# The last stage of a two-layer transformer kernel: choosing tokens in four partition quadrants and in two halves

## The chip, the cores and the metric

The kernel runs on one core of a Trainium2 chip. The core has five engines, each with its own instruction stream, worked in order: PE (TensorE, matmuls and transposes), DVE (VectorE), ACT (ScalarE), POOL (GpSimd) and SP (SyncE, which here only issues DMAs). They wait for each other by semaphores. The metric is device microseconds of one execution. The kernel before took 2501.3 us, the median of 3 runs (2497.42 to 2508.35).

## The reference

Four sequences of 1024 tokens with 256 features go through two layers. Layer 0 (windowed attention, then a feed-forward network with two of eight experts per token) and the attention of layer 1 (16 heads, normalised output) matter here only because they run before. The change is in the feed-forward part of layer 1, where experts choose tokens:

```python
gate_logits = jnp.einsum('bnd,de->bne', x, gate_w)
competitive_gates = sinkhorn(gate_logits)            # 8 rounds over tokens, then over experts
vals, idx = jax.lax.top_k(jnp.swapaxes(competitive_gates, -1, -2), M)   # M = 1024 / 8 = 128
...
routed = x[b_idx, routed_indices]
outputs = jnp.einsum('ebmd,edf->ebmf', routed, experts)                 # 8 experts, 256 x 256
outputs = outputs * jnp.transpose(gate_values, (2, 0, 1))[..., None]
routed_back = jnp.zeros_like(x).at[b_idx, routed_indices].set(vals_bmed)
```

Here x is the layer-normalised input, and the result is added to the input. Each of 8 experts takes the 128 best tokens of each sequence. Where several experts take one token, one row remains: that with the highest slot number, among equals that of the highest expert.

## The kernel before

Tokens stand in 32 tiles of 128 (x_t). The sequences form two groups: group 0 has sequences 0 and 1 (tiles 0 to 15), group 1 has 2 and 3. A group has 16 rows of (sequence, expert) with 1024 gate values each. The steps for a group, with the functions that give them:

- gate_steps (L1014) normalises a tile (xng, L1024, on POOL), stores it to DRAM (xn_d, L1027) and computes its gate logits (transposes L1038, matmuls L1048, clip L1055).
- share_steps (L1064) does eight rounds of scaling by sums over tokens (matmul L1075) and over experts; all between are small DVE operations.
- choose_steps (L1088) turns the gates to 16 rows of 1024 (L1100) and then, 16 times, finds the eight largest (L1109), their positions (L1111) and overwrites them with -1 (L1115), all on DVE. Three long operations per round make 47 in all. The 128 values and positions are transposed into columns, one per (sequence, expert): slot_gate, slot_tok and slot_row (L1123 to L1130).
- experts_on (L1135) gathers the chosen rows of xn_d, 128 rows per gather, by indirect DMAs that POOL issues (L1143), transposes two at a time (L1181), copies them (ACT, L1185), multiplies by the expert (L1154), scales by the gate (ACT, L1164) and stores to DRAM (y_d, issued by SP, L1168). Six xg buffers.
- The ranks say which slot of which expert holds a token. For group 0 they are scattered to DRAM (rank_d, POOL, L1597, 16 DMAs) and read back (read_ranks, L1234). For group 1 they are made on the core: hot (DVE, L1832) is a row of ones and zeros, place == slot, and one-hot matmuls against slot_col (L1834) sum slot numbers into rank_ps.
- back (L1194) finds each token's row of y_d in eleven small DVE steps (L1202 to L1219), gathers the rows (POOL, L1225), adds x (L1231; on POOL for group 0, on DVE for group 1) and stores to the output (SP, L1232).

Group 0's gates, shares, choice and scatters run inside the attention loop of layer 1 (the loop over p, 32 pairs of heads, and k, 8 steps), a step at a time (some, L1624; step, L1615; the lists between, gating, sort and aside). In that loop the maxima of a later pair are made ahead (maxima, L1423: matmuls L1429, reduced on DVE to tops, L1436) and go through DRAM (tops_d, L1453, and back, L1458); scores (L1471), their exponential on ACT (pT, L1479) and the sums (L1486) follow. finish (L1540) normalises the attention's output tiles on POOL (L1559 to L1564). With lag 0, the call of the last tile, finish and gate_steps run without fill between.

After the loop, group 1's shares, choice, experts, ranks and back follow, with group 0's experts and back given beside the choice: the code takes three steps of choose, then experts_on(0), 24 more steps, back(0), and the rest of choose. Each engine's order is made when the kernel is built, by a list scheduler: among the instructions that its own model holds ready it takes the one that was given first. Hence the order in which the Python code gives the work, and the buffers it has, decide the order in each engine's stream; tc.issue_after and paced tie an instruction to the newest one of another engine. DMAs wait in the stream of the engine that issues them, so that a store that waits for its data holds up what stands behind it on SP.

## Time and profile before

| what | us |
|---|---|
| median of 3 runs | 2501.3 (2497.42 to 2508.35) |
| the profiled execution | 2505.83 |
| its span | 2504.1 |
| PE, DVE, ACT, POOL busy in the span | 2273.6, 1392.9, 985.6, 632.2 |
| last gates of group 1 clipped (L1055) | at 2357.18 |
| last share round ends, choice of group 1 begins (L1091) | at 2378.86 |
| first and last long operation of that choice | 2381.85, 2440.7 |
| group 1's gathers of xn_d, first and last issue | 2442.77, 2462.94 |
| group 1's gathers of y_d, first and last issue | 2477.94, 2497.00 |

The page's line of 40 slices shows which engine is busy where, in tenths, and the clock that the throttle granted PE:

```profile
PE   6999999799999999999888999999999999998434
DVE  5455545524321222222476877777777798995393
ACT  1333333312111222222114666666666565666311
POOL 2233333510440000000333221212122211124455
PEclk8999999899999999999999999999999999999667
```

One slice is 62.6 us, so the last three are the stage that the change is about. "Idle before" names the instruction that released an engine after an idle time; "issue" is time in which an engine waited for nothing that the profile shows. In the chain of what ended last, each row is a start, a duration and what ran.

### The profile page before, as it was taken

What the parts mean: (1) busy time and instruction counts of PE and PEld (TensorE: products, weight loads), DVE (VectorE), ACT (ScalarE), POOL (GpSimd) and SP (SyncE); (2) the same over time, 40 slices, a digit from 0 to 9 for tenths busy, and PEclk for the clock granted to TensorE, in tenths of its full rate; (3) what the DMA queues carried; (4) which work ended last, traced back from release to release, by engine and by line L of the source; (5) the groups of instructions that cost most, each with busy time, mean ns of one, the idle gap of its engine ahead of it and who ended that gap; (6) DMA issues with size and microseconds to landing.
All of it is one profiled execution on the core that took longest, in us unless ns stands there. A gap on an engine that the chain in (4) does not pass through costs nothing.

```text
span 2504.1 us, 42234 instructions
## 1 busy us (share of the span) xinstructions
PE 2273.6 (91%) x16844; PEld 1352.2 (54%) x16844; DVE 1392.9 (56%) x2304; ACT 985.6 (39%) x1354; POOL 632.2 (25%) x728
## 2 busy tenths in 40 slices
PE   6999999799999999999888999999999999998434
PEld 3566666566557888887444444444444444443222
DVE  5455545524321222222476877777777798995393
ACT  1333333312111222222114666666666565666311
POOL 2233333510440000000333221212122211124455
PEclk8999999899999999999999999999999999999667
DMA  3000000420116666664515221313121313100144
GB/s 93 19 11 11 11 13 9 133 74 1 66 63 200 217 206 209 213 207 156 117 44 120 59 69 45 69 45 69 45 69 45 69 44 69 44 19 11 56 122 135
DMA packets 201744, 204.90 MB, mean 82 GB/s; under 512 B 90200, under 2 KB 162392, under 8 KB 201548
## 3 DMA queue, kind: packets, MB, share of 16 engines
q1 hardware_dynamic: 179148, 162.13, 22.7%
q0 software_dynamic: 11584, 29.72, 4.0%
q10 hardware_dynamic: 10816, 10.36, 1.2%
q8 instruction: 133, 2.18, 0.4%
q14 instruction: 63, 0.52, 0.1%
HBM read 140.70 MB, written 56.96 MB: 79 GB/s over the span
## 4 chain that ended last, share of the span: by engine, by line
PE 69%; DVE 16%; issue 6%; ACT 4%; POOL 3%; DMA 3%; SPq 0%; DVEq 0%; ACTq 0%; POOLq 0%
PE two L962 10%; PE two L1471 9%; PE acc L1486 8%; PE two L717 6%; DVE tops L1436 5%; PE two L329 5%; PE two L1429 4%; PE acc L989 4%; PE two L258 3%; PE two L1351 2%; PE two L321 2%; PE acc L735 2%; PE misc L735 2%; PE acc L396 2%; PE misc L440 1%
## 5 line engine op out<-in xcount | busy, mean ns | idle before, releaser
L1436 DVE TENSOR_REDUCE tops<-two 128x2 f32<-128x1024 f32 x512 | 619.5, 1217 | 103.8 <-PE two L1429 101.6
L1479 ACT ACTIVATE pT<-two 128x1024 f32<-128x1024 f32 x512 | 523.4, 1025 | 303.7 <-PE two L1471 299.2
L1486 PE MATMUL acc<-pT,v_t 128*32 128x256 f32 x4096 | 342.7, 393 | 5.8 <-ACT pT L1479 5.6
L1471 PE MATMUL two<-q_st,k_st 64*128 64x512 f32 x1024 | 259.8, 499 | 19.3 <-ACT pT L1479 11.8
L962 PE MATMUL two<-xbT,w_t 128*128 128x256 f32 (+1 forms) x1280 | 260.0, 358 | 1.3 <-ACT xbT L951 0.7
L717 PE MATMUL two<-xnT_f,w_t 128*128 128x512 f32 x512 | 234.7, 608 | 7.4 <-DVE tops L1436 5.1
L962 PEld LDWEIGHTS two<-xbT,w_t 128*128 128x128 f32 x1280 | 224.1, 192 | 32.0 <-ACT xbT L951 5.3
L1429 PE MATMUL two<-k_st,q_st 64*128 64x512 f32 x1024 | 220.3, 403 | 4.2 <-DVE glu L726 1.6
L1471 PEld LDWEIGHTS two<-q_st,k_st 64*128 64x128 f32 x1024 | 96.8, 184 | 209.8 <-issue 118.8
L1659 POOL DMA_INDIRECT yr<-ys_d,slot x64 | 62.6, 979 | 573.5 <-DMA w_raw<-in_L_attn_wk_dram 434.7
L1471 PE MATMUL two<-top_st,minus 64*128 64x512 f32 x1024 | 206.5, 396 | 0.0
L978 DVE SCALAR_TENSOR_TENSOR glu_b<-two,b_blk,act_b 128x256 f32<-128x256 f32 (+1 forms) x160 | 72.6, 453 | 235.8 <-ACT act_b L972 235.8
L972 ACT ACTIVATE act_b<-two,b_blk 128x256 f32<-128x256 f32 (+1 forms) x160 | 72.1, 451 | 312.6 <-PE two L962 161.1
L1486 PEld LDWEIGHTS acc<-pT,v_t 128*32 128x32 f32 x4096 | 86.5, 108 | 166.1 <-issue 142.8
L717 PEld LDWEIGHTS two<-xnT_f,w_t 128*128 128x128 f32 x512 | 96.7, 195 | 116.4 <-issue 104.4
L989 PE MATMUL acc<-w_t,glu_b 128*128 128x256 f32 x568 | 148.6, 390 | 8.0 <-DVE glu_b L978 3.7
L355 DVE TENSOR_REDUCE top<-two 128x4 f32<-128x768 f32 (+1 forms) x128 | 112.5, 919 | 69.0 <-PE two L329 69.0
L381 POOL TENSOR_SCALAR_AFFINE_SELECT pT<-pT 128x1024 f32<-128x1024 f32 x64 | 70.5, 1102 | 296.5 <-ACT pT L378 296.5
L725 ACT ACTIVATE act<-two,bT 128x512 f32<-128x512 f32 x64 | 44.0, 687 | 254.0 <-PE two L717 251.2
L1429 PEld LDWEIGHTS two<-k_st,q_st 64*128 64x128 f32 x1024 | 103.2, 185 | 73.5 <-ACT pT L1479 22.0
L378 ACT ACTIVATE pT<-two 128x768 f32<-128x768 f32 (+1 forms) x128 | 93.7, 783 | 119.0 <-PE two L329 118.6
L989 PEld LDWEIGHTS acc<-w_t,glu_b 128*128 128x128 f32 x568 | 102.1, 189 | 34.7 <-DVE glu_b L978 23.3
(317 smaller groups left out, 3095.0 us busy)
## 6 DMA issues: line engine op xcount, KB each, us to landing
w_t<-in_L_ffn_rw_dram SPq DMA_DIRECT2D x120, 512.0 KB
halves<-split SPq DMA_DIRECT2D x64, 256.0 KB
q_st<-halves SPq DMA_DIRECT2D x128, 128.0 KB
k_st<-halves SPq DMA_DIRECT2D x256, 64.0 KB
xb<-xs_d SPq DMA_DIRECT2D x31, 256.0 KB
ys_d<-yb ACTq DMA_DIRECT2D x31, 256.0 KB
xs_d<-zeros SPq DMA_DIRECT2D x5, 1536.0 KB
b_t<-in_L_ffn_rb_dram SPq DMA_DIRECT2D x40, 128.0 KB
```

The costliest lines, as they stand in the source:

```text
L329: mm(parts[r][:, gg, :], lhsT=left[32 * r : 32 * r + rows, g, l0 : l0 + P], rhs=right[32 * r : 32 * r + rows, g, r0 : r0 + n], start=(mask ...
L355: nc.vector.tensor_reduce(tops[i][:, 2 * ab : 2 * ab + 2, 2 * gp : 2 * gp + 2], scs[ab], AX.X, ALU.max)
L378: nc.scalar.activation(pt[:, 2 * ab : 2 * ab + 2, :, :n], scs[ab], AF.Exp)
L717: mm(ps[:, n * 512 : (n + 1) * 512], lhsT=w_t[:, kc, f * P : (f + 1) * P], rhs=xnT[:, kc, cols], start=(kc == 0), stop=(kc == 1),)
L735: mm(ps[:, jj * D : (jj + 1) * D], lhsT=glu[:, f, j * P : (j + 1) * P], rhs=w3_t[:, f, :], start=(f == 0), stop=(f == NF - 1),)
L962: mm(ps[:, m * 512 + ff * cols : m * 512 + (ff + 1) * cols], lhsT=w_t[:, kc, f * P : (f + 1) * P], rhs=xbT[:, kc, :cols], start=(kc == 0), ...
L989: mm(ps[:, a * D : (a + 1) * D], lhsT=glu[:, f, a * P : (a + 1) * P], rhs=w3_t[:, f, :], start=(f == 0), stop=(f == NF - 1),)
L1429: mm(sc[:, hh], lhsT=q_st[rows, j * P : (j + 1) * P], rhs=k_st[rows, kk * 512 : (kk + 1) * 512], start=True, stop=True,)
L1436: newest["vector"] = nc.vector.tensor_reduce(tops[:, :, j, kk], sc, AX.X, ALU.max).ins
L1471: mm(sc[:, hh * 512 : (hh + 1) * 512], lhsT=minus[rows] if top else k_st[rows, k * P : (k + 1) * P], rhs=(top_ring[p % 2] if top else q_st ...
L1479: newest["scalar"] = nc.scalar.activation(pt, sc, AF.Exp).ins
L1486: newest["tensor"] = mm(oT_ps[32 * r : 32 * r + 32, hh * D : (hh + 1) * D], lhsT=vals[n // HU][:, n % HU, k, :], rhs=pts[r // 2][:, hh * 5 ...
```

## The change

- Choice: the gate rows are put twice on 32 partitions, and the work array has four column blocks on four quadrants of 32 partitions. Round k puts its eight values into quadrant k // 4, and writes the array with them replaced into the place of the next round, so that the array of each round stays. One lookup then finds positions for all quadrants of a column at once: four lookups for 16 rounds. With parts = 2 (group 1) the first half of the slots (64 per expert) is given after eight rounds, with four lookups of its own, and the second half after the last. The columns come from small matmuls; slot_gate is copied by ACT. A column of a half holds 64 slots each of two experts.
- Gathers: take_rows issues all rows of a group or half at once, from 16 xg buffers.
- Order after the loop: group 0's 16 gathers, group 1's share rounds, group 0's experts, the sources of group 0, then choose of group 1; after its first eight steps, six pieces of group 0's way back; after the first half of the choice, its gathers, half_experts and ranks; eight more pieces of the way back; the rest of the choice; the second half's gathers, two pieces, and per sequence the ranks, experts and way back.
- half_experts multiplies two half columns as 64-wide column tiles of PE, one expert each, and stores 64 rows at a time (32 stores instead of 16 for group 1).
- Ranks: the one-hot rows of the first half are made on ACT (Abs, then Relu), those of the second half on DVE; rank_ps, sources and back go by sequence.
- The last tile's finish and xng run on DVE instead of POOL (lag 0). Six yr0 buffers instead of seven.

```diff
--- before.py
+++ after.py
...
-            t = pool.tile([P, D], F32, tag="yr0", name="sb3_k", bufs=7)
+            t = pool.tile([P, D], F32, tag="yr0", name="sb3_k", bufs=6)
...
-            nc.gpsimd.tensor_scalar(
+            (nc.gpsimd if lag else nc.vector).tensor_scalar(
...
-    def choose_steps(g: int, bank, chosen, after):
-
-        by_tile = gpool.tile([P, TB, GE], F32, tag="by_tile", name="by_tile", bufs=1)
-        nc.vector.tensor_copy(
-            by_tile.rearrange("p t (b e) -> p t b e", b=GB),
-            gates[:, g * GT : (g + 1) * GT, :].rearrange("p (b t) e -> p t b e", b=GB),
-        )
+    def choose_steps(g: int, bank, chosen, after, parts: int = 1):
+        by_tile = gpool.tile([P, TB, 2, GE], F32, tag="by_tile", name="by_tile", bufs=1)
+        for n in range(2):
+            nc.vector.tensor_copy(
+                by_tile[:, :, n].rearrange("p t (b e) -> p t b e", b=GB),
+                gates[:, g * GT : (g + 1) * GT, :].rearrange("p (b t) e -> p t b e", b=GB),
+            )
         yield 0
+        cur = gpool.tile([P, 4, S], F32, tag="cur", name="cur", bufs=1)
...
+        for k in range(rounds):
+            q, a = of_round(k)
+            behind(nc.vector.max, out=top_v[q, a, :], in_=cur[q, a, :])
             yield 0
+            if k + 1 < rounds:
+                q1, a1 = of_round(k + 1)
+                behind(
+                    nc.vector.match_replace,
+                    out=cur[q1, a1, :], in_to_replace=top_v[q, a, :], in_values=cur[q, a, :],
+                    imm_value=-1.0,
+                )
                 yield 0
+            if (k + 1) % (rounds // parts):
+                continue
+            part = (k + 1) * parts // rounds - 1
+            rows = slice(part * P // parts, (part + 1) * P // parts)
+            for a in range(4):
+                behind(
+                    nc.vector.max_index,
+                    out=top_i[rows, a, :], in_max=top_v[rows, a, :], in_values=cur[rows, a, :],
+                )
+                yield 0
+            behind(nc.vector.tensor_copy, top_f[rows], top_i[rows])
+            ps = bank()
+            n = GE // parts
+            for k0, top in enumerate((top_v, top_f)):
+                for j in range(part * 4 // parts, (part + 1) * 4 // parts):
+                    q = slice(32 * j, 32 * j + 32)
+                    for h in range(parts):
+                        row = 64 * h + 32 * (j % 2) if parts == 2 else 32 * j
+                        mm(
+                            ps[row : row + 32, k0 * n : (k0 + 1) * n],
+                            lhsT=top[q].rearrange("p a i -> p (a i)"),
+                            rhs=ident[q, 32 * j + h : 32 * j + GE : parts],
+                            start=True,
+                            stop=True,
+                        )
+            slot_gate = gpool.tile([P, n], F32, tag=f"slot_gate{part}", name="slot_gate", bufs=1)
+            slot_tok = gpool.tile([P, n], F32, tag=f"slot_tok{part}", name="slot_tok", bufs=1)
+            slot_row = gpool.tile([P, n], I32, tag=f"slot_row{part}", name="slot_row", bufs=1)
+            nc.vector.tensor_copy(slot_tok, ps[:, n : 2 * n])
+            nc.vector.tensor_copy(slot_row, slot_tok)
+            nc.scalar.copy(slot_gate, ps[:, :n])
+            chosen[g, part] = slot_gate, slot_tok, slot_row
+            after()
+            yield 1
...
+    def half_experts(g: int, part: int, m: int, xgs, pool, w_all):
+        slot_gate = chosen[g, part][0]
+        xgT = turned(xgs, pool)
+        ps = two_banks()
+        for c in range(2):
+            for kc in range(2):
+                for h in range(2):
+                    half = slice(64 * h, 64 * h + 64)
+                    mm(
+                        ps[half, c * D : (c + 1) * D],
+                        lhsT=xgT[:, 2 * c + kc, half],
+                        rhs=w_all[:, (2 * (m + c) + h) % E, kc, :],
+                        start=(kc == 0),
+                        stop=(kc == 1),
+                    )
+        for c in range(2):
+            b = (m + c) // (E // 2)
+            yg = pool.tile([P, D], F32, tag="yg", name="yg", bufs=4)
+            nc.scalar.activation(
+                yg, ps[:, c * D : (c + 1) * D], AF.Copy, scale=slot_gate[:, m + c : m + c + 1]
+            )
+            for h in range(2):
+                row = ((2 * (m + c) + h) % E) * CAP + 64 * part
+                nc.sync.dma_start(
+                    out=y_d[g * GB + b][row : row + 64, :], in_=yg[64 * h : 64 * h + 64, :]
+                )
+    def sources(rank, n: int):
...
+        return src_row
+    def back(b: int, src_row, n0: int, adder, queue, rows):
+        for t in range(TB):
+            i = b * TB + t
+            yr = rows.tile([P, D], F32, tag="yr", name="yr", bufs=16)
             nc.gpsimd.indirect_dma_start(
                 out=yr[:, :],
                 out_offset=None,
+                in_=y_d[b][:, :],
+                in_offset=bass.IndirectOffsetOnAxis(ap=src_row[:, n0 + t : n0 + t + 1], axis=0),
+            )
+            adder.tensor_tensor(yr, yr, x_t[i], ALU.add)
             queue.dma_start(out=out_rows[i * P : (i + 1) * P, :], in_=yr)
+            yield
 
...
+                v = nc.gpsimd if lag else nc.vector
+                v.tensor_scalar(
                     ys[j], ys[j], mv[:, j, 0:1], rstd[:, j : j + 1], ALU.subtract, ALU.mult
                 )
-                nc.gpsimd.tensor_tensor(ys[j], ys[j], gamma_b, ALU.mult)
-                nc.gpsimd.tensor_tensor(ys[j], ys[j], beta_b, ALU.add)
-                nc.gpsimd.tensor_tensor(x, x, ys[j], ALU.add)
+                v.tensor_tensor(ys[j], ys[j], gamma_b, ALU.mult)
+                v.tensor_tensor(ys[j], ys[j], beta_b, ALU.add)
+                v.tensor_tensor(x, x, ys[j], ALU.add)
...
-            yr = pools["yr"].tile([P, D], F32, tag="yr0", name="yr0", bufs=7)
+            yr = pools["yr"].tile([P, D], F32, tag="yr0", name="yr0", bufs=6)
...
+        slot_col = wpool.tile([P, 2, E // 2, E], BF16, name="slot_col")
...
+        columns = [(n // E, n) for n in range(GE)]
+        xgs = take_rows(chosen[0, 0], columns, pool)
         run(share_steps(1, one_bank, 0))
+        experts_on(0, xgs, pool, w_all)
+        src_row = sources(read_ranks(), GT)
+        rest = iter(
+            [back(b, src_row, b * TB, nc.gpsimd, nc.sync, pool) for b in range(GB)]
+        )
+        def some_back(n: int, now=[next(rest)]):
+            with tc.issue_after(newest["rows"]):
+                while n and now:
+                    if next(now[0], now) is now:
+                        now[:] = [j for j in (next(rest, None),) if j]
+                    else:
+                        n -= 1
+        columns = [(GB + m // (E // 2), m) for m in range(E)]
+        rank_ps = two_banks()
+        ready = []
+        choose = choose_steps(1, one_bank, chosen, lambda: ready.append(0), 2)
+        def ranks_of(part: int, m: int, on_scalar: bool):
+            tok = chosen[1, part][1][:, m : m + 1]
+            hot = pool.tile([P, S], BF16, tag="hot", name="hot", bufs=3)
+            if on_scalar:
+                far = pool.tile([P, S], F32, tag="far", name="far")
+                nc.scalar.activation(far, place, AF.Abs, bias=minus_tok[:, m : m + 1])
+                nc.scalar.activation(hot, far, AF.Relu, bias=1.0, scale=-1.0)
+            else:
+                nc.vector.tensor_scalar(hot, place, tok, None, ALU.is_equal)
+            b, mb = divmod(m, E // 2)
+            for hf in range(2):
+                mm(
+                    rank_ps[32 * b : 32 * b + E, hf * 512 : (hf + 1) * 512],
+                    lhsT=slot_col[:, part, mb, :],
+                    rhs=hot[:, hf * 512 : (hf + 1) * 512],
+                    start=(part == 0 and mb == 0),
+                    stop=(part == 1 and mb == E // 2 - 1),
+                )
+        for _ in range(8):
             next(choose)
+        some_back(6)
+        while not ready:
             next(choose)
+        minus_tok = wpool.tile([P, E], F32, name="minus_tok")
+        nc.scalar.mul(minus_tok, chosen[1, 0][1], -1.0)
+        xgs = take_rows(chosen[1, 0], columns, pool)
+        for m in range(0, E, 2):
+            half_experts(1, 0, m, xgs[m : m + 2], pool, w_all)
+            for c in range(2):
+                ranks_of(0, m + c, True)
+            next(choose)
+        some_back(8)
         run(choose)
+        xgs = take_rows(chosen[1, 1], columns, pool)
+        some_back(2)
+        backs = []
+        for b in range(GB):
+            for m in range(b * E // 2, (b + 1) * E // 2, 2):
+                for c in range(2):
+                    ranks_of(1, m + c, False)
+                half_experts(1, 1, m, xgs[m : m + 2], pool, w_all)
+            mine = slice(32 * b, 32 * b + E)
+            rankT = pool.tile([P, S], F32, tag="rankT", name="rankT")
+            nc.scalar.copy(rankT[mine], rank_ps[mine, :])
+            ps = one_bank()
+            for t in range(TB):
+                nc.tensor.transpose(
+                    ps[:, t * E : (t + 1) * E], rankT[mine, t * P : (t + 1) * P],
+                    ident[mine, mine],
+                )
+            rank = gpool.tile([P, TB, E], F32, tag="rank1", name="rank1")
+            nc.scalar.copy(rank.rearrange("p n e -> p (n e)"), ps[:, : TB * E])
+            run(back(GB + b, sources(rank, TB), 0, nc.vector, nc.sync, pool))
```

169 lines of the change are left out of this document (57 added, 112 removed).

## The prediction

> **What bounds the kernel now.** I read the table of the span by stages first, the chain of what ended last second, then groups and timelines of single stages. The table's columns are stretch, its length, busy time of PE, weight loads, DVE, ACT and POOL, granted clock, DMA share, GB/s.
>
> ```profile
> 2010.00:2280.00 270.00, 254.59 (x2173) 118.21 (x2172) 246.09 (x336) 167.12 (x186) 49.48 (x59) 0.99 0.16 41
> 2280.00:2340.00 60.00, 48.70 (x391) 20.66 (x391) 11.14 (x32) 42.71 (x49) 39.32 (x43) 0.92 0.06 15
> 2340.00:2358.00 18.00, 9.28 (x31) 6.58 (x32) 5.26 (x24) 2.19 (x6) 9.42 (x13) 0.50 0.30 93
> 2358.00:2381.00 23.00, 6.23 (x24) 4.73 (x24) 14.60 (x49) 0.00 (x0) 4.75 (x5) 0.50 0.21 66
> 2381.00:2442.00 61.00, 20.20 (x99) 16.92 (x99) 59.09 (x83) 11.07 (x24) 36.01 (x42) 0.67 0.42 125
> 2442.00:2478.00 36.00, 29.54 (x136) 18.39 (x135) 13.87 (x28) 12.02 (x26) 16.72 (x17) 0.93 0.40 117
> 2478.00:2504.00 26.00, 0.00 (x0) 0.00 (x0) 6.84 (x16) 0.00 (x0) 15.38 (x16) 0.50 0.56 162
> ```
>
> To 2340 us PE sets the pace (attention). Then four stages, each with one owner: gate rounds 2358 to 2381 (a DVE and PE chain), the choice for group 1 to 2442 (DVE 59.1 of 61 us), ranks and experts to 2478 (POOL's gathers, then PE), the way back (POOL's gathers, PE idle). The chain gives the joints (start, duration, what):
>
> ```profile
> 2335.70 0.72 POOL y L1563
> 2357.18 0.18 DVE gates L1055
> 2378.86 0.24 DVE by_tile L1091
> 2381.85 1.23 DVE top_v L1109
> 2383.10 1.27 DVE top_i L1111 x2
> 2384.38 1.21 DVE cur L1115
> 2440.73 0.23 DVE top_f L1121
> 2477.94 0.94 POOL yr L1225
> 2500.77 0.43 DVE yr L1231
> ```
>
> A round of the choice is 1.25 + 1.28 + 1.23 = 3.76 us; 16 rounds fill 2381.85 to 2440.7. From the first yr gather to the end of the span: 26.2 us. Beside the rounds PE runs group 0's experts:
>
> ```profile
> 2381.02 1.11 PE L1181 MATMUL acc<-ident,xg 128*128 128x128 f32 x4
> 2381.93 1.06 PE L1181 MATMUL misc<-ident,xg 128*128 128x128 f32 x4
> 2382.85 2.86 PE L1154 MATMUL two<-w_all,xgT 128*128 128x256 f32 x8
> 2385.55 0.60 PE L1181 MATMUL acc<-ident,xg 128*128 128x128 f32 x4
> ```
>
> All eight pairs take 21.0 us (to 2402.0): 1.11 + 2.86 = 4.0 for the first, at granted clock 0.5 (the clock row shows 1.0 from 2384.64), 2.16 for later ones. They cost nothing today because DVE is longer. That cover is what the change takes away.
>
> **The attention part (to the gates of the last tile).** Three edits reach it.
> 1. Group 0's choice has 12 fewer long DVE operations (16 + 15 + 4 lookups for 47). Pairs of heads without these operations take about 27.5 us, with five about 29.5: 0.35 us of PE time each, so 12 x 0.35 = 4.2 us gained around 2200 to 2260. But group 0's rank table is now read, and its key (first step of the sources) computed, inside the loop: in the changed order key stands on DVE ahead of the maxima of the next to last pair (before about 2256), and waits for the sixteenth scatter of ranks. Those 16 scatters move from 2277-2338 to about 2196-2260; the last issues at about 2255.4 by the exponential it is tied to, lands in 2.2 us, the read takes 2.24 (both from this trace): data at 2260.0, DVE there at 2253.6. Behind key wait the maxima, so PE, for up to 6.4 us, less what PE has in hand; on SP the maxima's table of the last pair (issued at 2260.27 now) waits behind the rank read too, about as late as key's data. I take gain and wait as cancelling (0; ends -3 and +3).
> 2. With the scatters (1.0 us + 0.3 each) gone from POOL's stretch 2280 to 2340, its normalisation finishes earlier. Today PE pays here:
>
> ```profile
> 2307.90 0.63 PE L1038 MATMUL misc<-ident,xng 128*128 128x128 f32 x4 [1.86 <-DVE ctx L1509]
> ```
>
> DVE itself had waited 10.7 us for POOL there, and after this idle time the granted clock is 0.5 from 2309.55 to 2316.38, about half of 6.8 us lost. x of the tile group comes about 2.4 us earlier, more than the 1.86. I take 4 us (0 to 5). POOL's y at 2335.70 had waited 0.7 for a scatter: +0.7.
> 3. The last tile's finish and xng go to DVE: 0.42 us and less for POOL's 1.23 + 3 x 0.72 and 1.24: but PE's and ACT's steps between stay, and the chain crosses two more queues; 1.5 us (0.5 to 3).
> Together 6.2 us earlier at the first gate round (0 to 11).
>
> **The tail, walked in today's times (the 6.2 us comes off at the end).**
> - Gate rounds as now, but the first pair of group 0's experts is ahead of the last round's matmul: +0.9, end 2379.7.
> - In PE's order of the changed kernel all eight expert pairs of group 0 now stand ahead of the transposes that start group 1's choice. They begin after the seventh round's matmul, 2374.95 (its 16 gathers, 1.25 each on POOL, are ahead of that), and take 21.0: to 2396.0. Transposes 1.0 at full clock, copies and waits 1.1: first MAX8 at 2398.15 instead of 2381.85, **16.3 us later**.
> - First half: 8 rounds of max and replace, 8 x 2.48 = 19.8; 4 lookups of 1.28 = 5.1, to 2423.1; conversions and the eight small matmuls (1.3 us for the two of today) taken as 3.15: slot rows at 2426.25. Today all slots are there at 2442.0.
> - First half's gathers from 2427.0: 8 x 1.25 = 10. POOL then has eight gathers and eight adds of group 0's way back, 15.0 us for the same work in today's trace: free at 2452.2.
> - Second half on DVE alone: 18.6 + 5.1 + 3 after 2426.25, about 2450 (2448 to 2453). But its slot matmuls stand on PE behind all eight one-hot matmuls of the first half, and those one-hots are now on ACT: two 1024-wide operations (1.02 each, by the 1024-wide exponential) for eight columns = 16.3, plus 4 copies of 0.59 and 8 of 0.47: 22.5 from about 2431, so 2453.8.
> - ACT is held up further: yg has four buffers, and the product that takes the fifth waits for writes that stand on SP behind out_dram of group 0 numbers 7 and 11, whose adds on POOL end at 2443.8 and 2450.45; the write lands 1.8 us after its issue (uncontended y_d rows). That puts the last one-hot at 2456.2, the second slot rows at 2457.8, the second half's gathers at 2458.5.
> - POOL from there: 8 x 1.25 = 10, two gathers and adds of group 0 (last add 2473.4). SP sends that add's result (0.33), then seven y_d writes (0.43 each; now 32 of 64 KB instead of 16 of 128 KB), to 2476.4; + 1.8 landing + 0.2 to the gather: first yr gather of group 1 at 2478.4 (2475.5 if ranks, not SP, were last). The second sequence's ranks and writes are covered by the first one's eight gathers (10 us).
> - From there 26.2 as now: 2504.6 against 2504.1, **+0.5** (ends -8 and +9: the former if nothing on ACT and SP holds the second half, the latter for longer ACT operations from SBUF and a slower pace of POOL beside DVE).
> Nothing is counted for: slot_gate on ACT (idle in the choice), six yr0 buffers for seven (each fetch has at least 3.5 us in hand), set-up of slot_col on POOL (beside the gate rounds; uncovered under 2 us), the sources of group 0 otherwise (DVE has room once its 11 steps, 2.74 us, are past the wait).
>
> [...] half_experts writes 64-column halves of PE. The trace has narrow tiles between full ones already: eight 32-column records (L1486) span 0.64 us, eight full-width ones (L1154) 1.89, and in 2300 to 2305 us they follow 64-row and full ones with no gap, starts 0.33 to 0.57 apart. [...] The sum goes by the row: at most today's 1.89 per pair. Second, the writes of 64 KB: the row is an SP issue of 0.43, so 16 more cost 6.9 us of SP's time, of which seven issues (3.0) lie on my path. [...] I keep 3.0, since the first half's writes are issued while ACT still works on its one-hots.
>
> **Rivals.**
> - *Faster: the second half is bound by DVE and POOL only.* For it: ACT is idle through 2358 to 2381 and busy 11 of 61 us in the choice; the SP hold-up rests on a hand walk. Against: SP's order has those writes behind out_dram. Then the gathers start when POOL is free, 2452.2; first yr 17.25 later (2469.5), end 2495.7: -8.4, with -6.2: -14.6 us, 2486.7.
> - *Slower: PE stays at half clock through group 0's experts.* They start in the gate rounds, where PE works 6.2 of 23 us and the clock is 0.5; today it rises 3.6 us after the experts begin, but DVE feeds nothing there, gathers come one per 1.25 us and the pairs would starve between them if POOL is late. At 4.0 per pair for 2.16, 8 x 1.84 = 14.7 us later start of the choice, all on the path: -6.2 + 0.5 + 14.7 = +9, 2510. From 5.7 us on it decides.
> - *The attention gives nothing:* key's wait on DVE costs PE its 6.4 and a stretch of half clock (3.4), which eats both gains. Speaks for it that PE's idle time of 1.79 us at 2256.6 was followed by clock 0.5 already. 6.2 is lost: +0.5, 2502.
>
> **How the numbers follow.** The profiled execution took 2505.8 us (span 2504.1 and 1.7 around it), the median of the runs is 2501.3; the sum -6.2 + 0.5 = -5.7 holds for both: 2495.6. A measurement can tell about 0.5%, 12.5 us. Chances: forecast 0.45 (own range 2489 to 2504; 0.04 of it beyond the bound to the fast side, 0.02 to the slow), faster rival 0.25 (0.22 beyond), half clock 0.20 (0.13 beyond, with a part of the attention's gain missing), no gain in attention 0.10 (0.05 beyond, with the tail's +9). So faster 0.26, within 0.54, slower 0.20. Range: 2483 (the faster rival less 4) to 2514 (the slower one plus 4).
>
> **What would show it.** Right: experts of group 0 on PE from about the seventh gate round; first MAX8 of group 1 some 16 us later after the gates than now; second slot rows some 31 us after the first; ACT waiting on y_d writes in between; no wait of 1.86 us at 2307.9; DVE idle before key. [...]

## The result, and the profile after

The changed kernel took 2525.52 us, the median of 4 runs (2524.94 to 2533.87); the kernel before beside it 2502.42 (4 runs). The ratio is 1.0103, 95% interval 1.0074 to 1.0131: **slower by 1%**, where 2495.6 was forecast. On another chip it came to 1.0061 (1.0037 to 1.0085). Ratios and intervals here are those of the record; the quotient of two medians can differ from them by up to 0.25%.

Whole times of one kernel differ by up to 1.3% (2491.94 to 2524.4 us in 31 executions of the kernel before). Much of it arises ahead of layer 1: its first exponential lies between 1316.5 and 1341.3 us in the traces (1332.5 and 1316.5 in two of the changed kernel), with 82 to 123 us at half clock before it (88 in the trace of the kernel before, 102 in the changed one's). So stages are compared from that exponential on. From there to the end of the last operation the kernel before takes 1175.3 us in its trace, the changed one 1196.3: 21.0 more. This table says where, and holds the experiments for later (us; steps between events of the trace; the gathers are the first of each half of group 1, before: the first and the ninth).

| stage | before | after | E1 | E2 | E5 | E6 | E9 | best, other chip |
|---|---|---|---|---|---|---|---|---|
| start of layer 1's loop (16 exponentials) | 37.2 | 40.5 | 41.4 | 40.5 | 41.3 | 40.5 | 37.0 | 37.1 |
| to pair 23 | 685.3 | 686.2 | 686.1 | 686.0 | 686.1 | 686.1 | 685.4 | 685.4 |
| pairs 23 to 26 | 131.6 | 142.9 | 140.7 | 133.1 | 140.6 | 140.6 | 131.6 | 131.6 |
| pairs 27 to 31 | 154.0 | 155.1 | 153.0 | 155.1 | 152.9 | 147.7 | 153.9 | 154.0 |
| last tile, to its gates | 23.4 | 22.2 | 22.2 | 22.9 | 22.2 | 22.2 | 22.0 | 22.0 |
| gate rounds, to the first maximum of group 1 | 24.5 | 41.3 | 24.7 | 40.9 | 40.3 | 41.1 | 24.7 | 24.6 |
| to the first half's gathers | 60.9 | 29.3 | 29.3 | 29.3 | 29.3 | 29.3 | 29.3 | 29.3 |
| to the second half's gathers | 10.8 | 32.2 | 32.2 | 32.2 | 26.1 | 32.3 | 34.0 | 26.6 |
| to the first way-back gather | 24.3 | 23.6 | 22.9 | 24.8 | 23.7 | 23.4 | 24.3 | 24.7 |
| to the last operation | 23.3 | 22.9 | 23.3 | 22.9 | 23.6 | 22.8 | 23.6 | 23.2 |
| sum | 1175.3 | 1196.3 | 1175.7 | 1187.8 | 1186.1 | 1185.9 | 1165.9 | 1158.4 |

The whole tail, gates to end, grew by 5.5 us; 16.6 came in the attention loop, where a gain was expected, and 1.2 went off the last tile. These are pairs 23 to 26 and 27 to 31 of the kernel before, then rows of the changed kernel's table by stages (columns as before):

```profile
2048.40:2180.00 131.60, 124.09 (x1054) 58.37 (x1052) 120.43 (x160) 79.75 (x91) 25.28 (x30) 1.00 0.23 54
2180.00:2334.00 154.00, 140.13 (x1176) 62.87 (x1174) 101.60 (x152) 101.66 (x113) 50.49 (x58) 0.97 0.08 20
```

```profile
2059.30:2202.10 142.80, 131.97 (x1054) 61.22 (x1052) 125.12 (x155) 79.82 (x90) 25.27 (x30) 0.94 0.20 50
2202.10:2357.20 155.10, 140.13 (x1190) 62.81 (x1188) 92.63 (x143) 101.35 (x113) 51.63 (x59) 0.94 0.08 20
2357.20:2379.50 22.30, 11.24 (x46) 7.50 (x46) 7.23 (x20) 5.28 (x11) 8.42 (x14) 0.56 0.29 96
2402.00:2420.80 18.80, 17.88 (x94) 15.29 (x92) 1.63 (x5) 10.14 (x23) 4.96 (x6) 0.93 0.36 113
2420.80:2450.10 29.30, 0.85 (x16) 0.60 (x16) 28.54 (x39) 2.05 (x4) 4.94 (x8) 0.57 0.16 54
2450.10:2482.30 32.20, 19.49 (x112) 8.78 (x113) 21.50 (x31) 20.18 (x28) 20.79 (x25) 0.71 0.45 127
2482.30:2505.90 23.60, 18.43 (x112) 8.81 (x111) 7.93 (x22) 8.01 (x16) 11.85 (x13) 0.84 0.37 101
2505.90:2532.20 26.30, 0.00 (x0) 0.00 (x0) 8.31 (x26) 0.00 (x0) 15.37 (x16) 0.52 0.59 175
```

Row 4 of the second table is the new stage: DVE works 1.6 of 18.8 us while PE runs group 0's experts. In row 6 no engine is busy for more than some two thirds of the time: a chain over several engines and SP sets it. And in rows 1 and 2, attention, the granted clock is 0.94, where the same pairs had 1.00 and 0.97. The chain of what ended last has the joints of the tail:

```profile
2397.10 1.13 PE acc L1196 x4
...
2415.55 3.46 PE two L1209 x16
2419.48 1.29 DVE cur L1109 x2
2420.79 1.23 DVE top_v L1126
...
2453.82 2.66 DMA xg<-xn_d,slot_row
...
2469.08 2.07 DMA y_d<-yg
2471.71 2.08 ACT far L1923 x2
2475.30 2.06 DMA y_d<-yg
2478.91 1.96 PE two L1929 x4
2484.98 1.22 POOL xg L1180
```

Experts stand ahead of the choice, and stores to y_d hold up ACT and so the second half, both as the prediction walked it.

### The profile page after: what moved, and what is told of

It reads as the page before. It is cut to its first block, busy times and chain, and to the rows that moved or that the text cites. A ratio compares the mean times of both kernels' runs of the same rounds, so it can differ in the third digit from the quotient of the medians.

```text
span 2532.2 us, 42466 instructions
## 1 busy us (share of the span) xinstructions
PE 2300.7 (91%) x16960; PEld 1361.2 (54%) x16960; DVE 1377.5 (54%) x2275; ACT 1002.4 (40%) x1376; POOL 626.0 (25%) x725
## 5 line engine op out<-in xcount | busy, mean ns | idle before, releaser
L989 PEld LDWEIGHTS acc<-w_t,glu_b 128*128 128x128 f32 x568 | 102.1, 190 | 34.7 <-DVE glu_b L978 23.3
```

The lines of the kernel that those rows point to most:

```text
L989: mm(ps[:, a * D : (a + 1) * D], lhsT=glu[:, f, a * P : (a + 1) * P], rhs=w3_t[:, f, :], start=(f == 0), stop=(f == NF - 1),)
```

## The experiments

**E1: the choice before the experts.** Theory: the 16.8 us that the first maximum comes later are the eight expert pairs of group 0, which stand ahead of the transposes on PE only because they are given first.

```diff
         run(share_steps(1, one_bank, 0))
+        ready = []
+        choose = choose_steps(1, one_bank, chosen, lambda: ready.append(0), 2)
+        for _ in range(3):
+            next(choose)
         experts_on(0, xgs, pool, w_all)
...
-        for _ in range(8):
+        for _ in range(5):
             next(choose)
```

> The first three steps of group 1's choice (by_tile, eight transposes, two copies) are given ahead of group 0's experts, so that on PE the transposes stand right behind the eighth gate round's matmul; nothing else moves. Theory T (the tail pays for experts of group 0 on the path of the choice): in the changed kernel the first MAX8 came 41.3 us after the last tile's gates against 24.5 before, 16.8 later; here 25 us after the gates, and the time falls from about 2525 to 2509 (-16). Rival: the tail is held by POOL and SP, which keep their order (the way back of group 0 must wait for its experts), so the second half's gathers move by 6 us or less and the time stays above 2518. The attention part has the same order as in the changed kernel: if its half-clock stretches come back at the same places, they belong to the order and not to chance.

Measured: 1.0018 of the kernel before (0.9985 to 1.0051); the median, 2514.64 us, lies between the 2509 of the theory and the rival's 2518. The first maximum is 24.7 us behind the gates, and the stages after it keep their lengths. The timeline of DVE at this place, the changed kernel first, then E1:

```profile
2419.48 0.68 DVE L1109 COPY cur<-acc 32x512 f32<-32x512 f32 x1 [17.14 <-PE acc L1104]
```

```profile
2399.29 0.68 DVE L1109 COPY cur<-acc 32x512 f32<-32x512 f32 x1 [1.20 <-PE acc L1104]
```

DVE's wait for the transposes falls from 17.14 to 1.20 us and the tail from 149.3 to 132.4. The experts themselves cost nothing then: they run beside the first rounds.

**E2 and E7: what slows pairs 23 to 26.** DVE has 28 long operations of the choice in these pairs in both kernels (the twelve that are saved fall later), and yet they take 9 to 11 us more. E2 gives group 0 the old choice back (16 rows on partitions 0 to 15, a lookup per round) and moves its sources behind the share rounds; group 1 and the arrays stay. E7 is E2 with one thing more: the same 16 rows stand on partitions 32 to 47.

```diff
-        cur = cur4[:GE, 0]
+        cur = cur4[32 : 32 + GE, 0]
...
-        top_v = cur4[:GE, 2, :CAP]
+        top_v = cur4[32 : 32 + GE, 2, :CAP]
...
-                nxt = cur4[:GE, (k + 1) % 2]
+                nxt = cur4[32 : 32 + GE, (k + 1) % 2]
```

> Group 0's choice is made as before (16 rows, three long operations a round, 47 in all), and the read of its ranks and its sources are held behind the last gate round; the rest, the whole tail too, is that of the changed kernel. Theory A (the loss ahead of the tail, about 17 us of the 23, comes from group 0's choice by quadrants and its ranks inside the attention loop): 2508 to 2511, that is before plus the tail's 6 us. Rival B (it comes from elsewhere, the start of the loop and six yr0 buffers, or from chance): 2520 to 2526.

> As the run with group 0's choice made as before (e2_old_choice0), but its 16 rows stand on partitions 32 to 47 instead of 0 to 15, with one more small copy at the end; the long operations, their number (47) and their places stay. Theory P (a DVE operation on partitions that do not begin at 0 no longer overlaps its neighbours: +30 ns of gap on either side where there were 70 ns of overlap): 0.2 us per operation, the stretch of pairs 23 to 26 (28 operations) grows from 133 to 138 or more with what PE then loses to the clock, and the gaps read +30 ns from the first operation on. Rival: the gaps come from the order edges or the 32 rows of the quadrant choice, then -70 ns and 133 us as in the run compared.

Measured: pairs 23 to 26 take 133.1 us in E2 and 141.5 in E7 (E2 as a whole 1.0065 of the kernel before, 1.0040 to 1.0091; E7, one run, 2547.63 us beside 2510.98). E2's median, 2523.36 us, is not the 2508 to 2511 of theory A but within its rival's 2520 to 2526: pairs 23 to 26 fell by 9.8 us, while the start of the loop (40.5), pairs 27 to 31 (155.1) and the tail kept what they had lost. Between E2 and E7 the work is the same, so the partitions make the difference; the chip does not, for E8 and E9 (further down), on the chip of E7, take 134.8 and 131.6 us there with the rows at partition 0. Two stretches of DVE's timeline show how, E2's and then E7's (start, duration):

```profile
2047.41 1.20 DVE L1557 TENSOR_REDUCE tops<-two 128x2 f32<-128x1024 f32 x1
2048.55 1.21 DVE L1112 MAX8 cur<-cur 16x8 f32<-16x1024 f32 x1
2049.68 1.20 DVE L1557 TENSOR_REDUCE tops<-two 128x2 f32<-128x1024 f32 x1
```

```profile
2071.22 1.23 DVE L1559 TENSOR_REDUCE tops<-two 128x2 f32<-128x1024 f32 x1
2072.48 1.22 DVE L1112 MAX8 cur<-cur 16x8 f32<-16x1024 f32 x1
2073.73 1.23 DVE L1559 TENSOR_REDUCE tops<-two 128x2 f32<-128x1024 f32 x1
```

In E2 each operation starts 0.06 to 0.08 us before the last has ended (2047.41 + 1.20 = 2048.61, next at 2048.55); in E7 it starts 0.02 to 0.03 after. The two operations together take 2.27 us in E2 and 2.51 in E7. Over all long operations of the choice the distance to what follows is -0.07 us in the kernel before and +0.03 in E7. In the changed kernel it is -0.07 as long as the rounds stay in quadrant 0 (to 2072 us) and +0.03 from the first write to partitions 32 and up. In pairs 23 to 26 that is 21 of the 28. Some 0.2 us for each is 4 us of DVE, in pairs where DVE is busy 36.7 of 41.9 us (23) and 27 to 29 of 29 to 31 (24 to 26). PE pays twice: its idle time in the four pairs grows from 7.5 to 10.8 us (7.2 in E2, 12.4 in E7), and its busy time, for the same 1054 records, from 124.1 to 132.0, since the clock is at 0.5 for 17 us of the stage and never in the kernel before. Together these are the 11.3 us. Not all of that half clock comes with the partitions. It has three stretches, which begin 24.4, 61.9 and 99.4 us into the stage. The first, of 6.83 us, stands in E8 too (24.9 us, 6.83), and for 3.41 us in E2 (24.7), both with all rows on partitions 0 to 15, and E7 has none there; PE has no idle time over 1.05 us ahead of it. So some 3 us of the 11.3 belong to what E8 shares with the changed kernel, and some 8 to the partitions, as E7 against E2 (8.4) says. What starts a stretch of half clock is not shown. That the rows are 32 instead of 16, or that edges between steps changed, is excluded: E7 has neither. What is not separated is whether it is the partition or a change of it: all these operations stood between reductions that begin at partition 0. Four lookups in a row that all begin at partition 64 do overlap (last section), which speaks for the change from one operation to the next.

**E6: where the scatters stand on POOL.** In pair 29 of the changed kernel PE stands still for 6.94 us. The timelines of POOL, DVE and PE there:

```profile
2275.78 0.72 POOL L1636 TENSOR_TENSOR y<-y,rows_b 128x256 f32<-128x256 f32 x1
2276.66 1.07 POOL L1670 DMA_INDIRECT rank_d<-place,at_i  x1 [0.17 <-issue]
...
2280.13 0.98 POOL L1670 DMA_INDIRECT rank_d<-place,at_i  x1 [0.15 <-issue]
2281.41 0.96 POOL L1670 DMA_INDIRECT rank_d<-place,at_i  x1 [0.30 <-issue]
2282.39 0.73 POOL L1602 TENSOR_TENSOR y<-y,rows_b 128x256 f32<-128x256 f32 x1
```

```profile
2283.16 0.42 DVE L1603 TENSOR_TENSOR y<-y,misc 128x256 f32<-128x256 f32 x1 [6.51 <-POOL y L1602]
2283.50 2.35 DVE L1507 TENSOR_REDUCE tops<-two 128x2 f32<-128x1024 f32 x2
2285.77 0.22 DVE L1270 TENSOR_SCALAR key<-rank 128x128 f32<-128x128 f32 x1
```

```profile
2284.77 0.80 PE L1542 MATMUL two<-q_st,k_st 64*128 64x512 f32 x2 [6.94 <-DVE tops L1507]
```

DVE waits 6.51 us for one small product of POOL, which stands behind the finish of four tiles and four rank scatters; the maxima and so PE stand behind DVE. key, named in the prediction as the one that would wait, comes 2.6 us later and does not wait. E6 gives one scatter per step, so that all are ahead of the finish (of tiles 24 to 27):

```diff
                 paced(sc.ins, newest["scalar"])
-                yield from wait(2)
+                yield from wait(1)
```

> Group 0's sixteen rank scatters are given one per step instead of one per two steps; on POOL all of them now stand ahead of the normalisation of tiles 24 to 27, and the key stands about 20 DVE instructions earlier. Theory A2 (the last four scatters, 5 us of POOL between the normalisation's steps, hold y and so PE, idle 6.94 us and then three stretches of half clock): the idle time falls to about 2, one stretch or none follows, the time falls by 5 to 9 us, 2516 to 2520. Rival: the wait moves to the key, which now stands earlier and waits for the read of the ranks: PE idles as long there, 0 to -2, 2523 to 2526.

Measured: pairs 27 to 31 in 147.7 us instead of 155.1 (152.9 and 153.0 in E5 and E1), the whole 1.0058 (1.0028 to 1.0088). DVE's wait at the same operation in E6:

```profile
2278.67 0.42 DVE L1603 TENSOR_TENSOR y<-y,misc 128x256 f32<-128x256 f32 x1 [0.83 <-POOL y L1602]
```

Against the kernel before (154.0) that is 6.3 us less, with twelve long operations fewer in these pairs as well. The scatters' own part is seen in pairs 30 and 31, which have no operation of the choice in either kernel: 62.2 us before (60.7 in its trace on another chip), 56.2 in E6 and in the changed kernel alike. So moving the scatters off the last pairs is worth 4.5 to 6 us, if they do not hold up POOL's other work on the way.

**E8: the start of the loop.** The first 16 exponentials take 40.5 to 41.4 us in every kernel with the large array of the choice among the loop's arrays; these kernels have six yr0 buffers too. E8 is the kernel before with an array of that size (of which it uses two rows of blocks) and with six yr0 buffers; its work is the same.

```diff
-        cur = gpool.tile([GE, S], F32, tag="cur", name="cur")
+        cur4 = gpool.tile([P, 4, S], F32, tag="cur", name="cur", bufs=1)
+        cur = cur4[:GE, 0]
```

> The kernel before with two sizes of the change alone: the choice's work array is a tile of 128 x 4 x 1024 in one buffer (of which the old choice uses two blocks of 16 rows), and six yr0 buffers. Theory L (the larger array moves the addresses of the pools, and so the order at the start of the attention loop, where the changed kernel lost about 3.5 us between the first and the second pair): 40.5 to 41.4 us from the first exponential to the seventeenth, 37.2 before, and all later stages as before. Rival (those 3.5 us are chance, or come from elsewhere in the change): 37 to 38.

Measured: 41.1 us there, 134.8 in pairs 23 to 26 (one run, 2517.13 us beside 2510.98). The two sizes cost 3.9 us at the start of the loop. The later stages did not all stay, as had been expected: pairs 23 to 26 are 3.2 us longer than before, by the one stretch of half clock named above, which stands at 24.1 to 24.9 us in eight of the nine traces with these sizes (not in E7) and in none of the five without them in the loop (the kernel before on two chips, E9, the best one, the second of E10). Whether the array or the sixth buffer does it was not separated. The order on PE differs at the end of the sixteen exponentials: in E8 products for v_t (L1392) stand ahead of the seventeenth exponential's scores, in the kernel before behind them. Why was not followed.

**E5: eight yg buffers.** Theory: the second half waits, over ACT's one-hots, for stores to y_d that stand on SP behind group 0's results, because yg has four buffers. SP's and ACT's timelines in the changed kernel:

```profile
2426.59 40.55 SPq L1302 DMA_DIRECT2D out_dram<-yr  x3
2467.23 2.44 SPq L1258 DMA_DIRECT2D y_d<-yg  x4
2469.76 3.67 SPq L1302 DMA_DIRECT2D out_dram<-yr  x4
```

```profile
2471.24 0.47 ACT L1253 ACTIVATE yg<-two,slot_gate 128x256 f32<-128x256 f32 x1 [0.36 <-DMA y_d<-yg]
2471.61 2.18 ACT L1923 ACTIVATE far<-place,minus_tok 128x1024 f32<-128x1024 f32 x2
2476.19 0.47 ACT L1253 ACTIVATE yg<-two,slot_gate 128x256 f32<-128x256 f32 x1 [2.40 <-DMA y_d<-yg]
```

```diff
-            yg = pool.tile([P, D], F32, tag="yg", name="yg", bufs=4)
+            yg = pool.tile([P, D], F32, tag="yg", name="yg", bufs=8)
```

> yg gets eight buffers instead of four, nothing else; the order on every engine is that of the changed kernel. Theory T2 (the second half's slot rows wait on ACT, which waits for y_d writes behind out_dram on SP): the 9.9 us that DVE idles ahead of the second slot rows shrink to 2 to 4, the second gathers start 6 to 8 us earlier and the time falls to 2517 to 2519. Rival: ACT's own work (16 one-hot operations of about 1.0 us, 22.5 us in all) is what holds it, then 0 to -2, 2523 to 2525. As the order is the same, the attention part shows what of its half-clock stretches repeats.

Measured: 26.1 instead of 32.2 us between the halves' gathers, no wait of ACT for y_d, 3.84 us of DVE's idle time ahead of the second slot rows instead of 9.92; the whole 1.0068 (1.0038 to 1.0097). The median, 2524.39 us, is not the 2517 to 2519 that were expected, though the stages of the trace add up to 10.2 us less; the step carries the argument here, not the whole. The stores still stand behind group 0's third batch of results on SP, but nobody waits for them.

**E9: what the runs suggest.** Group 0's choice as before, group 1's in halves with its arrays in another pool, E1's order, E5's buffers, seven yr0.

```diff
-                    choose_steps(0, misc_bank, chosen, chose)
+                    choose_whole(0, misc_bank, chosen, chose)
...
-        choose = choose_steps(1, one_bank, chosen, lambda: ready.append(0), 2)
+        choose = choose_steps(1, one_bank, chosen, lambda: ready.append(0), 2, wpool)
```

> The changed kernel's tail with two edits (the first steps of group 1's choice ahead of group 0's experts; eight yg buffers), and the attention part of before: group 0's choice as before, seven yr0 buffers, group 1's work array in the last stage's own pool; the last tile's finish stays on DVE. Order in the attention loop is that of before. Theory T with T2: from the last tile's gates to the end 126 us instead of 143.9, with 1.2 less ahead of it, so 17 to 19 us below before, a ratio of 0.992 to 0.994. Rival: the two gains of the tail do not add up, because POOL's gathers and group 0's way back are next in line: 9 to 12 us below before.

Measured: 2506.2 us beside 2510.98, 0.9972 (0.9951 to 0.9994), less than even the rival's gain. Loop start and pairs are the old ones, as they should be, but the step between the halves took 34.0 us, as if yg still had four buffers. The timelines of PE and ACT show something else:

```profile
2436.75 1.95 PE L1290 MATMUL two<-w_all,xgT 128*64 128x256 f32 x16
```

```profile
2445.52 0.84 ACT L1300 ACTIVATE yg<-two,slot_gate 128x256 f32<-128x256 f32 x2 [6.10 <-remote]
```

PE's records of these products end at 2438.70, PE's next signal in the trace comes at 2445.50, three at once, and ACT, which waits for them, starts at 2445.52. The store that its buffer had needed was issued by 2410.49, 35 us earlier (SP's first twelve to y_d, 11.62 us from 2398.87).

**E10: three repairs with quadrants kept, and E9 with the scatters of E6.** The first is the changed kernel with the edits of E1, E5 and E6; the second is E9 with the edit of E6.

> The changed kernel with three repairs and nothing undone: three steps of group 1's choice given ahead of group 0's experts, eight yg buffers, one rank scatter per step instead of two. Quadrants stay in both groups. Nothing is left out. Stages are counted from the first exponential of layer 1 (the kernel before: 1175.3 us to the end, the changed one 1196.3). If the three repairs act independently of each other: loop start 41, pairs up to 22 686, pairs 23 to 26 still 141 (the writes off partition 0 stay), last pairs 148, last tile 22, then 24.7 to the first maximum, 29.3 to the first half's gathers, 26.1 to the second half's, 23 and 23.5 to the end: 1164.6, that is 11 us under the kernel before. If the earlier choice puts the first half's stores behind group 0's results on SP again, as the last kernel's trace suggests (step between the two halves' gathers 34.0 in spite of eight buffers): 32 to 34 there and 1171 to 1173, 3 us under it. If the last pairs keep their 155 whatever the scatters do: 1172 to 1180.

> The last kernel (choice of group 0 as before, arrays of group 1's choice in another pool, early choice, eight yg buffers, seven yr0) with one rank scatter per step instead of two. Nothing is left out. With the choice of group 0 twelve operations longer, its scatters begin later than in the kernel with quadrants, and in the order written for POOL they stand among the finish of tiles 24 to 27 and of the next four. If what counts is that they leave the last pairs: e432 to e511 148 instead of 153.9, and 1150 to 1160 us from the first exponential to the end (1165.9 without the edit). If what counts is that they are ahead of the finish, they aren't here, and the wait moves: 154 to 160 in that stage, 1166 to 1172. The step between the two halves' gathers tells here too whether the 34.0 of the last kernel comes again (a cause in the order) or was one execution's (26 to 27).

Measured: 2514.31 us, 1.0015 (0.9996 to 1.0035), and 2509.8 us, 1.0002 (0.9985 to 1.0020), beside 2510.34; from the first exponential 1180.7 and 1173.0 us. In the second the last pairs take 161.0 us instead of 153.9: with the old, longer choice the dense scatters fall on the finish, and what DVE waits for there (x of POOL) grew from 10.7 us in the kernel before to 13.4. The scatters' place counts, not that they are early. In the first the last pairs took 152.0 (148 was expected with all three): 6.8 us of half clock at 2220.62, which E6 had not, account for 3.4 of the 4. And both had 36 to 37 us between the halves, with the wait of E9 (7.2 and 7.8 us "remote").

**E12: is that wait the order's or the chip's?** The kernel before, the best one (E9's code) and the changed one, traced on one chip, another than E9's and E10's; nothing in them is edited.

> The kernel before itself, for a trace from the same chip as the next two. Open is why the combined kernels show 34 to 37 us between the two halves' gathers where eight yg buffers alone had 26: in their traces ACT waits 6 to 8 us for products whose records on PE ended long before. If that is a trait of the chip that those runs fell on, this kernel shows such waits in its last stage too, there: 26 to 28 from the first gather of the second eight to the first way-back gather instead of 24.3, and PE's signals late or missing in the trace. If it comes from the changed order, this kernel has its old stages (24.5, 60.9, 10.8, 24.3, 23.3).

> The combined kernel that was ahead of the kernel before (choice of group 0 as before, early choice of group 1 with its arrays in another pool, eight yg buffers, seven yr0), with the kernel before and the changed one traced on the same chip. If the wait of ACT is a trait of the chip and this one hasn't got it: 26 to 27 between the halves' gathers, some 1158 us from the first exponential of layer 1 to the end, 0.993 of the kernel before. If it is the order: 34 to 37 again, 1166, and 0.997. If it is the chip's and this chip has it: 34 to 37 here, and the other two are longer in their last stages as well.

> The changed kernel itself on the same chip: 1.010 of the kernel before within the interval had before, and its stages 41, 686, 141 to 143, 155, 22, 41, 29, 32, 24, 23 again, if these belong to the kernel. With the late signals of PE on this chip, 35 to 40 between the halves' gathers.

Measured: the best kernel 2492.46 us beside 2508.45, **0.9912 (0.9881 to 0.9944)**, the changed one 2526.5, 1.0061 (1.0037 to 1.0085). The wait is absent in all three. The quotient of the best kernel's medians is 0.9936. Rows of the best kernel's table by stages: pairs 23 to 26, then the tail from the first maximum on:

```profile
2053.30:2184.80 131.50, 124.03 (x1054) 58.38 (x1052) 120.43 (x160) 79.71 (x90) 25.27 (x30) 1.00 0.22 54
...
2385.40:2414.70 29.30, 18.31 (x110) 15.54 (x108) 28.52 (x39) 12.77 (x28) 9.88 (x13) 0.85 0.38 126
2414.70:2441.20 26.50, 18.54 (x112) 8.69 (x113) 21.75 (x32) 19.90 (x28) 20.84 (x24) 0.76 0.42 122
2441.20:2466.00 24.80, 18.85 (x112) 9.05 (x111) 8.28 (x27) 7.81 (x16) 12.81 (x13) 0.81 0.46 131
```

Clock 1.00 and DVE's 120.43 us in the first row; in the second PE works 18.3 us beside DVE's 28.5, where the changed kernel had 0.85. From the first exponential the best kernel takes 1158.4 us and the kernel before 1175.4, so the order alone does not make E9's wait. E8 says more: with the order of the kernel before in its last stage and four yg buffers, on the chip of E9, ACT waited in the same way, and the step to the first way-back gather took 27.4 us instead of 24.3:

```profile
2470.65 0.84 ACT L1165 ACTIVATE yg<-two,slot_gate 128x256 f32<-128x256 f32 x2 [3.07 <-remote]
```

So the wait is in all three traces of that chip (E7, E8, E9, each with another order of the last stage) and in both of E10's chip, and in none of the four of E1, E2, E5 and E6 and the three of E12, on two other chips. As far as these twelve traces show, it goes with the chip. Its cause stays open.

## Why the prediction was wrong, point by point

The forecast was -6.2 for the attention and +0.5 for the tail. The traces gave +15.4 (the loop's 16.6 less 1.2 of the last tile) and +5.5.

- **Group 0's choice ("gain and wait as cancelling, 0; ends -3 and +3").** This step failed, and the largest part of the miss is here. The price of 0.35 us of PE time per operation was taken from operations on partitions 0 to 15. For the operations that were saved it held: pair 28, with none instead of five, took 27.9 us for 29.7. But it was carried to those that stay, on partitions 32, 64 and 96, where the same operation has no overlap with its neighbours on DVE: 8.4 us by E7 against E2, of the +11.3 in pairs 23 to 26. The bounds did not hold because both ends assumed the trace's price of an operation to stay; the trace of before had no row off partition 0 beside maxima, so the price was unknown and had to be bounded as such.
- **key's wait.** This did not come: key found the rank data in place. A wait of the size named (6.4; measured 6.51) came in DVE's queue ahead of it, from POOL; that the sizes agree is chance. The prediction named what stands behind key on DVE and SP, but walked the sixteen scatters past POOL's own queue only at the place they leave, not at the place they go to.
- **Scatters gone from 2280 to 2340 us (4 us, POOL's y 0.7).** The wait of 1.86 us before the transposes of xng is gone indeed, and its half clock too; the gain came, 4.5 to 6.0 us in pairs 30 and 31 (against the two traces of the kernel before) for the 4.7 named. The scatters took it back where they went: pair 29 took 36.1 us for 30.0 (31.5 in the other trace), and with a stretch of half clock in pair 27 the stage ends at +1.1. E6, without that wait, has -6.3.
- **Costed at nothing: six yr0 buffers and the large array.** Loop start +3.3, and some 3 in pairs 23 to 26. The fetches were argued, the array's place in memory was not mentioned. E8 shows that these two sizes alone do it, 3.9 and 3.2; which of the two, it does not show.
- **Last tile on DVE (-1.5).** Measured -1.2.
- **Start of the choice (16.3 us later).** Measured 16.8, by the walk's own chain; E1 takes it off.
- **First half (28.85 us).** Measured 29.3. **Second half behind ACT and SP (31.5 us).** Measured 32.2, and E5 shows the ring: -6.1. The faster rival needed that chain absent; in E5 it is, and the step is 26.1 where that rival's own times (2427.0 to 2452.2) gave 25.2. Of what the tail's end of +9 stood for, the longer ACT operations came: the one-hots took 1.13 to 1.15 us (L1923) and 1.04 to 1.06 (L1924) for 1.02. A slower pace of POOL beside DVE is not shown: in the changed kernel's trace POOL's sixteen adds took 0.71 to 0.75 us (L1301), with DVE busy and without.
- **From there to the first way-back gather (19.9 us).** Measured 23.6, the tail's one mis-sized term. SP's 0.33 us for the last result was named and left out of the sum (2473.4 + 0.33 + 3.0 is 2476.7, not 2476.4). The stores of 64 rows take 0.59 to 0.63 us each on SP (15 in 9.40), not the 0.43 of 128 rows, and land in 2.1 to 2.8 us, not 1.8: seven of them 1.4 longer, the landing 0.3 to 1.0, the last add of group 0 up to 1.2 later behind the second half's gathers.
- **Two other sums.** The second half on DVE alone, 18.6 + 5.1 + 3 after 2426.25, is 2453.0 and not about 2450; nothing hung on it, since ACT was later. The ends of the attention's terms add up to -1.8 and 11.7, not 0 and 11.
- **Half clock through group 0's experts (the slower rival).** Not so: the eight pairs took 21.9 us (2397.10 to 2419.01) for the forecast's 21.0; from the fourth on they are 2.17 us apart, at full clock.
- **Column tiles and stores of half the rows.** For the columns the row held but for little: 16 records of 64 columns, two at a time, take 1.89 to 1.95 us at full clock, 8 full ones 1.89. But the reading "no gap" was too coarse. Behind a 64-column record the first one of another shape starts 0.31 us after it, behind a full product 0.22 (a full product or a transpose); behind the transposes the first 64-column one starts after 0.20, a full one after 0.11. That is 0.09 us per change, some 1.5 us of PE time in sixteen changes (an estimate from these rows). For the stores the prediction's row was too low: in a run of stores one of half the rows takes SP 0.59 to 0.63 us, one of all rows 0.45 in the same trace.

The measured 2525.5 us lies 11 above the upper bound of 2514. The chances put 0.20 on slower, most of it on the tail's half clock, which did not come; the attention's end of +3 was too near, since all rows behind it were rows of the old shape.

## What to carry to other kernels

A long DVE operation is priced with its neighbours: read starts against ends, and expect the price to change when rows move to other partitions than their neighbours' (here from 2.27 us for two operations in E2 to 2.51 in E7). Work given earlier is walked through the queues that it joins, not only those that it leaves; four scatters of 1.0 us each among the work ahead of one small product made DVE wait 6.5 us for it, and PE with it; without them it waited 0.8. And of a change with many parts, some parts may be good: here the two halves of group 1's choice, given ahead of the experts, with eight buffers, and the last tile on DVE were worth 0.9% (17.0 us by stages) once group 0's choice was left as it was, on a chip without the wait that E9 showed; on one with it 0.3%.

## What the runs showed that was not expected

- In these traces DVE operations of 1.2 us on rows from partition 0 start 0.07 us before the last one ends (the kernel before); on 16 rows at partition 32 (E7), or 32 rows at 32, 64 or 96 (the changed kernel), with such neighbours, they start 0.03 after it, and last 0.01 us longer. The lookups over all 128 partitions overlap again (-0.08), and so do those of the second half on 64 rows from partition 64 (2466.17 + 1.23 = 2467.40, the next starts at 2467.32), where the neighbours begin at partition 64 as well.
- In the trace of the kernel before and in that of the changed one the changes of the granted clock lie whole multiples of 3.41 us apart, and from 1400 us to the end of the loop the stretches at 0.5 last 3.41, 6.83 or 10.24 us. No size of idle time settles in these two traces when one comes: of the eleven there, four began 1.2 to 2.4 us after the end of idle times of PE of 1.23, 1.49, 1.79 and 1.86 us, one inside that of 6.94, and six (two of them from 2083.61 and 2223.56 us in the changed kernel) have none over 1.2 ahead; none began within 7 us after those of 1.42 and 1.43 (two in each trace). One at the same place of the program came in eight of nine traces (E8).
- On two chips ACT waited in the last stage for PE's products in a way that the profile puts down to "remote": 5.42 us in E7, 6.10 in E9, 7.20 and 7.81 in the kernels of E10, 3.07 in E8. In E9 ACT began 6.82 us after PE's records of the work had ended. On two other chips, on one with E9's code, no trace has such a wait (E1, E2, E5, E6 and the three of E12).
